# The four key quarters of the attention's sum, added by a TensorE fold or by an exchange through DRAM

## The chip, the cores and the metric

The kernel runs on one core of a Trainium2 chip. The metric is the time of one execution on the device, in microseconds (us). Engines are named as in the profile: PE is TensorE, DVE is VectorE, ACT is ScalarE, POOL is GpSimd, and SP is the engine that issues nearly all transfers. All data are float32. On PE each float32 matrix product shows in the trace as two passes, so a product of the program counts as two matmuls there.

## What is computed

One transformer block with adaptive layer norms, for 4 sequences of 1024 tokens, width 512, 16 heads of 32 with one shared key and value head (k_w and v_w have 32 rows), and a gated FFN of width 2048 with Walsh-Hadamard transforms:

```python
sa, ca, ga, sb, cb, gb = (silu(c) @ wmod) per sequence    # ga, gb kept away from zero
h = layernorm(x) * (1 + ca) + sa
q = (h @ q_w.T + q_b).reshape(b, s, 16, 32);  k = h @ k_w.T + k_b;  v = h @ v_w.T + v_b
attn = softmax(causal(q . k / 32 ** 0.5))
x = x + ga * ((attn @ v).reshape(b, s, 512) @ o_w.T + o_b)
h = layernorm(x) * (1 + cb) + sb
u = fwht(h * SU_ug) / 64
u = silu(u @ W_gate.T * wg) * (u @ W_up.T * wu)
x = x + gb * (fwht(u * SU_dp) / 64 @ W_down.T * wd)
```

## The kernel before

The 4096 tokens are handled in 8 blocks of 512 (half a sequence each), in the order given by `order`; a block is two halves of 256 tokens or four tiles of 128. For each block the attention side runs first norms, K, V and Q projections, scores, exponentials, transposes, the product with V, the output projection, the addition to x and the second norm; the FFN side then runs gate and up products (a Strassen form, L1054, with mixtures of the weights made on POOL, L1018) and down products (L1192) for that block. The FFN of one block runs beside the attention of the next ones.

No queue order is written by hand. Each part is a generator (a stream) that yields operations with an engine, a planned cost and the buffers that it reads and writes; `Flow` keeps a model of when each engine is free, and always emits the operation that could begin first, and among those of the same engine within 0.3 us the one with the lowest rank in the list at the end of `adaln_block` (L1234 ff.). Every engine then executes its instructions in the order in which they were emitted. So a changed cost, wait or rank changes the whole order. The model gives a transfer 3.9 us per MB, one after another, plus 1.5 us, and a change of PE's form (`mode`: full, rows, cols, tiles) 0.16 us.

The parts that the change touches:

- `fronts` projects K, V and Q from hT. `qT` holds the scaled Q^T of a whole block, 512 tokens (`[128, 4, 512]`). A half is projected when `st.scored >= (i - 1) * NT + 2 * (hf + 1)`, that is, when the same half of the block before has been used up (L416). The copies from PSUM are L428.
- `scores` (L500) makes the scores of a tile in row groups (each head's 32 channels lie on a quarter of the partitions); `minima` (L524, DVE), `exps` (L547, ACT), `reciprocals` (L561, DVE), `scales` (L581, ACT) and `turns` (L596, DVE transpose) follow.
- `attend` (L624) multiplies with V. The transpose leaves the keys of each group of 32 in place, so the product is made for each of four partition groups (quarters of the keys) by itself, in 32x32 tiles of PE, and comes out in four PSUM banks: 128 partitions = four groups of 32 channels for the four key quarters. ACT copies the four banks to `oT` (L637), a half tile (8 heads) at a time. There is one `oT`, and the copies of the next half tile wait for `st.folded >= qn`.
- `finish` adds the four key quarters: a product with `fold` (four stacked unit matrices, 128x32) in the four column groups of PE, L660, which also puts the heads on the partitions as the output projection needs them. ACT copies the result to `aT` (L663). After the second half tile comes the output projection (L297 with ow, aT), and DVE multiplies with the gate (L677).
- `add` (L692, L694) adds the gated result to x on POOL; from block 3 on, `transformed` does the first Walsh-Hadamard transform on POOL (L731).
- `load` (L286) issues all transfers on SP. The weights stream through small rings: wd three buffers, wu three, wg two, each 256 KB.

Of the kernel before, what the change touches and what calls it, by code (L numbers as in the profile page):

```python
# [17 lines left out]
H, HD = 16, 32  # L18
# [142 lines left out]
def adaln_block(ctx, tc, x_d, small_d, const_d, wmod_d, qwT_d, kwT_d, vwT_d, vb_d, owT_d, ob_d,  # L161
# [8 lines left out]


    ROWS, VIA_DRAM = 3, 4
    ps = psum.tile([P, 8, 512], F32, name="ps")

    def sb(name, *shape):
        return outer.tile([P, *shape], F32, name=name)
# [2 lines left out]
    wd_d = dram.tile([NFC, P, D], F32, name="wd_d")  # L179

    gates_d = dram.tile([5, B, D], F32, name="gates_d")
    xT_d = {"a": dram.tile([NHALF, D, HB], F32, name="xTa_d"), "f": dram.tile([NHALF, D, HB], F32, name="xTf_d")}
    rows = [slice(HD * j, HD * j + HD) for j in range(4)]

# [33 lines left out]
    vT = sb("vT", HB)  # L218
    vrep = sb("vrep", NKV * TB // 32, HD)
    hT = sb("hT", NDC, HB)  # L220
    qT = sb("qT", NDC, TB)

    bt = sb("bt", 7, 2, HB)
    B11, B12, B21, B22, T1, T2, T4 = range(7)
# [6 lines left out]
    NNM = 12  # L231
    nm = sb("nm", NNM, 2, 4)
    den = sb("den", 4, H)
    oT = sb("oT", 4, H // 2, 32)
    rden = sb("rden", 4, H)
    aT = sb("aT", NDC, P)
    ga, obga, y = sb("ga", D), sb("obga", D), sb("y", D)
# [43 lines left out]
    def until(queue, name):  # L281
        return lambda: bool(queue) or name in over
# [6 lines left out]
    def bk(b):  # L289
        return ("bank", b)  # L290

    def act_cost(n):
        return 0.285 + 0.00083 * n
# [95 lines left out]
    def fronts(blocks):  # L389
        for i in blocks:  # L390
            kv = kv_slot[order[i]]
            for hf in range(2):
                hh = 2 * i + hf
                yield lambda: st.first_normed > hh

                yield lambda: st.attended_blocks >= kv_behind[i]
                yield banks.have(1)
                o, = banks.take(1)
                yield Op("PE", mm(HB, 4), lambda: full_mm(
                    ps[:, o, 0:HB], [(kvw[:, k, :], hT[:, k, :]) for k in range(NDC)]),  # L400
                    [("hT", 0), ("hT", 2), "kw0", ("kw", 64), ("kw", 96)], [bk(o)], mode="full")
# [13 lines left out]

                yield lambda: st.scored >= (i - 1) * NT + 2 * (hf + 1)  # L416
                yield banks.have(2)
                bb = banks.take(2)
                for o, c0 in zip(bb, (0, 2)):
                    def products():  # L420
                        for c in (c0, c0 + 1):
                            full_mm(ps[:, o, (c - c0) * HB:(c - c0 + 1) * HB],
                                    [(qw[:, k, c * P:(c + 1) * P], hT[:, k, :]) for k in range(NDC)])
                    yield Op("PE", mm(HB, 8), products, [("hT", 0), ("hT", 2), "qw"], [bk(o)], mode="full")
                st.fronts = hh + 1
                for o, c0 in zip(bb, (0, 2)):
                    for c in (c0, c0 + 1):
                        yield Op("ACT", act_cost(HB), lambda: nc.scalar.activation(  # L428
                            qT[:, c, hf * HB:(hf + 1) * HB], ps[:, o, (c - c0) * HB:(c - c0 + 1) * HB], AF.Identity,
                            bias=qbs[:, c:c + 1], scale=HD ** -0.5), [bk(o)], [("qT", c, hf)])  # L430
                    banks.give(o)
                st.ready = hh + 1

# [53 lines left out]
    def scores():  # L487
        for u in units:
            yield lambda: st.ready > 2 * u.i + u.ql // 2
            yield lambda: st.attended >= u.behind  # L490

            for cs, kb, n in u.visits():
                yield lambda: len(to_min) < 2
                yield banks.have(4)
                bb = banks.take(4)

                def products():
                    for m, c in enumerate(cs):
                        for j, r in enumerate(rows):
                            nc.tensor.matmul(ps[:, bb[j], m * n:(m + 1) * n], qT[r, c, u.ql * P:(u.ql + 1) * P],  # L500
                                             kT[r, u.kv[kb] * TB:u.kv[kb] * TB + n], start=True, stop=True)
                yield Op("PE", mm(n, len(cs)) + 0.1, products,
                         [("qT", c, u.ql // 2) for c in cs] + [("kT", j) for j in u.half_keys(kb, n)],
                         [bk(b) for b in bb], mode="rows")
                to_min.append((u, cs, kb, n, bb))
            if u.h0 + u.heads == H:
                st.scored += 1
        over["scores"] = True
# [90 lines left out]
                to_attend.append(u)  # L599
        over["turns"] = True  # L600

    to_finish, to_add, to_norm, to_gate = deque(), deque(), deque(), deque()

    def attend():


        while True:
# [24 lines left out]
            for h0 in range(0, u.heads, 8):  # L632
                half = (u.h0 + h0) // 8
                qn = 2 * (u.i * NT + u.ql) + half
                yield lambda: st.folded >= qn
                for g in range(4):
                    yield Op("ACT", act_cost(HB), lambda: nc.scalar.copy(  # L637
                        oT[:, g], ps[:, bb[g], h0 * 32:h0 * 32 + HB].rearrange("p (h q) -> p h q", q=32)),
                        [bk(bb[g])], ["oT"])
                    if h0 + 8 == u.heads:  # L640
                        banks.give(bb[g])
                to_finish.append((u.i, u.ql, half))
            if u.h0 + u.heads == H and u.ql == NT - 1:
                st.attended_blocks = u.i + 1
        over["attend"] = True

    def finish():

        while True:
            yield until(to_finish, "attend")  # L650
            if not to_finish:
                break
            i, ql, half = to_finish.popleft()
            yield banks.have(1)
            bo, = banks.take(1)

            def folds():
                heads = oT.rearrange("p g (c j) q -> p j c g q", c=2)
                for j, r in enumerate(rows):
                    nc.tensor.matmul(ps[r, bo, 0:HB], fold, heads[:, j], start=True, stop=True)  # L660
            yield Op("PE", 0.5, folds, ["oT"], [bk(bo)], mode="cols")
            st.folded += 1
            yield Op("ACT", act_cost(HB), lambda: nc.scalar.copy(  # L663
                aT[:, 2 * half:2 * half + 2, :], ps[:, bo, 0:HB].rearrange("p (c q) -> p c q", c=2)), [bk(bo)], ["aT"])
            banks.give(bo)
# [12 lines left out]
            banks.give(o)  # L678
            to_add.append((i, ql))
        over["finish"] = True  # L680
# [550 lines left out]
    def early(rank, later):  # L1231
# [1 line left out]

    ranked = [  # L1234
        (0, copies), (0, sums), (0.5, multiply), (1, outputs), (0.2, load_weights_once), (2, load_jobs), (2, mods),
        (early(1.8, 3), attend), (early(1.8, 3), finish), (early(1.8, 3), add), (3.5, transformed), (early(2.2, 4), minima), (early(2.05, 4), scores), (early(1.7, 5), second_norms), (0, lambda: first_norms([0])), (0.1, lambda: first_norms([1])), (2.1, lambda: fronts([0])),
        (6.1, lambda: first_norms(range(2, NHALF))),
        (6, lambda: fronts(range(1, NBLK))), (early(2.3, 7), turns), (early(2.5, 8), exps), (1.5, reciprocals), (early(2.4, 7.5), scales), (2.6, butterflies),
        (2.15, transforms), (0.3, mixes), (9, hand_over), (10, lambda: load_gu("wu", 3, wupT_d)), (10, lambda: load_gu("wg", 2, wgT_d)), (10, load_wd),
# [54 lines left out]
```

## Time and profile before

| what | value |
|---|---|
| runs | 2073.97, 2070.32, 2072.89 us; median 2072.89 |
| profiled execution | 2072.41 us, of which the span of the core is 2070.6 |
| mean granted clock of PE | 0.993 of full speed |
| L660 (fold), PE | 512 matmuls, 41.3 us busy, 395 ns each |
| L663 (copy to aT), ACT | 64 copies, 24.5 us, 383 ns each |
| L637 (copies to oT), ACT | 256 copies, 78.5 us, 383 ns each |
| L624 (product with V), PE | 8256 matmuls, 196.5 us busy |
| L1192 (down), PE | 1024 matmuls, 480.9 us |
| L1054 (gate and up), PE | 3584 matmuls, 903.6 us |
| transfers | 226.8 MB, mean 110 GB/s; the packets of SP's queue took 37.3% of 16 engines' span |

Busy times are those of one profiled execution. An engine's busy share is an average over the span. "Idle before" a group is time in which its engine had nothing to do until the group began, with the instruction that ended it. The chain that ended last is followed back from the last instruction, at each step to what released it. A matmul row counts passes that overlap when they use different parts of PE, so the 512 fold matmuls of 395 ns each are busy for 41.3 us only.

### The profile page before, as it was taken

How to read it: one execution, taken by the hardware profiler on the slowest of the kernel's cores; microseconds unless marked ns; L12 is line 12 of the kernel's file. 1: busy time of each engine (PE TensorE's matmuls, PEld its weight loads, DVE VectorE, ACT ScalarE, POOL GpSimd, SP SyncE). 2: the span in 40 equal slices, each digit the busy share in tenths (PEclk: the TensorE clock that was granted, in tenths of full speed). 3: DMA queues.
4: the chain of work that ended last, by engine and by line, in shares of the span. 5: the costliest groups of instructions: out<-in, count | busy, mean ns of one | idle time of the engine just before them, and what ended most of it. 6: DMA issues, size and time to landing. Idle time of an engine off the chain costs nothing.

```text
span 2070.6 us, 41956 instructions
## 1 busy us (share of the span) xinstructions
PE 1992.2 (96%) x16168; PEld 1272.1 (61%) x16168; DVE 1361.6 (66%) x3131; ACT 1150.5 (56%) x2447; POOL 863.1 (42%) x1134
## 2 busy tenths in 40 slices
PE   6898999999999999999999999999899999999998
PEld 4466666556665665646666566665566646664774
DVE  4985666676773776767875787775866758772331
ACT  3756765566664774646654675567744646650220
POOL 2582333223331455533563155252665346254441
PEclk9899999999999999999999999999999999999999
DMA  6145423432233453343333642243433344235333
GB/s 211 40 141 152 129 82 92 115 116 73 77 98 112 134 126 101 104 140 107 84 90 99 167 114 89 70 133 100 125 82 87 93 123 123 68 92 163 107 104 114
DMA packets 328144, 226.77 MB, mean 110 GB/s; under 512 B 108020, under 2 KB 266868, under 8 KB 327944
## 3 DMA queue, kind: packets, MB, share of 16 engines
q1 hardware_dynamic: 324008, 221.65, 37.3%
q8 instruction: 128, 2.10, 0.4%
q10 hardware_dynamic: 3936, 2.43, 0.4%
q14 instruction: 72, 0.59, 0.1%
HBM read 191.47 MB, written 32.55 MB: 108 GB/s over the span
## 4 chain that ended last, share of the span: by engine, by line
PE 86%; DVE 5%; DMA 3%; issue 2%; POOL 2%; SPq 1%; ACT 0%; ACTq 0%; POOLq 0%; DVEq 0%
PE ps L1054 36%; PE ps L1192 19%; PE ps L297 11%; PE ps L624 9%; PE ps L500 7%; PE ps L660 2%; DVE p L596 1%; DVE p L524 1%; POOL u L731 1%; DMA raw<-in_wmod 1%; PE ps L962 1%; POOL xr L731 1%; DVE g L1167 1%; SPq L286 1%; PE ps L965 1%
## 5 line engine op out<-in xcount | busy, mean ns | idle before, releaser
L1192 PE MATMUL ps<-wd,g 128*128 128x512 f32 x1024 | 480.9, 604 | 12.1 <-DVE g L1167 9.1
L547 ACT ACTIVATE p<-p,nm 128x512 f32<-128x512 f32 (+7 forms) x512 | 390.9, 766 | 25.9 <-DVE nm L524 25.5
L1054 PE MATMUL ps<-bt,ws 128*128 128x256 f32 x1536 | 380.4, 384 | 7.0 <-DVE rden L561 4.6
L581 ACT ACTIVATE p<-p,rden 128x640 f32<-128x640 f32 (+7 forms) x480 | 349.5, 783 | 39.0 <-DVE rden L561 38.3
L596 DVE STREAM_TRANSPOSE p<-p 128x512 f32<-128x512 f32 (+7 forms) x256 | 341.3, 1357 | 41.1 <-ACT p L581 38.4
L1141 DVE TENSOR_TENSOR s<-ps,s 128x256 f32<-128x256 f32 x384 | 159.8, 420 | 266.6 <-PE ps L1054 201.3
L1054 PEld LDWEIGHTS ps<-bt,ws 128*128 128x128 f32 x1536 | 290.4, 191 | 68.6 <-issue 16.6
L1192 PEld LDWEIGHTS ps<-wd,g 128*128 128x128 f32 x1024 | 185.0, 189 | 237.8 <-issue 186.2
L524 DVE CUSTOM_DVE_ANT_0 p<-ps,maskw 128x512 f32<-128x512 f32 (+3 forms) x512 | 276.6, 581 | 53.0 <-PE ps L500 52.2
L1018 POOL TENSOR_TENSOR ws<-wu 128x256 f32<-128x256 f32 x128 | 103.8, 811 | 476.6 <-DMA wu<-in_wupT 461.5
L1054 PE MATMUL ps<-bt,wu 128*128 128x256 f32 x1024 | 270.9, 387 | 1.0 <-issue 0.7
L1054 PE MATMUL ps<-bt,wg 128*128 128x256 f32 x1024 | 252.3, 383 | 3.4 <-issue 3.4
L1054 PEld LDWEIGHTS ps<-bt,wu 128*128 128x128 f32 x1024 | 188.0, 190 | 92.1 <-issue 49.2
L1054 PEld LDWEIGHTS ps<-bt,wg 128*128 128x128 f32 x1024 | 193.3, 191 | 59.6 <-issue 30.6
L624 PE MATMUL ps<-p,vrep 32*32 32x256 f32 (+1 forms) x8256 | 196.5, 415 | 20.4 <-issue 11.4
L1157 ACT ACTIVATE th<-s,wgh 128x512 f32<-128x512 f32 x128 | 92.4, 722 | 178.5 <-DVE g L1167 103.1
L500 PE MATMUL ps<-kT,qT 32*128 32x512 f32 (+3 forms) x1536 | 177.1, 528 | 1.4 <-ACT vT L409 1.4
L624 PEld LDWEIGHTS ps<-p,vrep 32*32 32x32 f32 x8256 | 120.7, 103 | 92.9 <-issue 40.2
L1132 ACT COPY s<-ps 128x256 f32<-128x256 f32 x128 | 47.5, 371 | 221.2 <-PE ps L1054 220.9
L637 ACT COPY oT<-ps 128x256 f32<-128x256 f32 x256 | 78.5, 383 | 137.3 <-PE ps L624 121.2
L1018 POOL TENSOR_TENSOR ws<-ws,wg 128x256 f32<-128x256 f32 x128 | 101.0, 789 | 114.8 <-DMA wg<-in_wgT 93.7
L694 POOL TENSOR_TENSOR xr<-xr,y 128x512 f32<-128x512 f32 x32 | 43.0, 1344 | 242.2 <-DVE y L677 238.6
(117 smaller groups left out, 2345.1 us busy)
## 6 DMA issues: line engine op xcount, KB each, us to landing
wd<-wd_d SPq DMA_DIRECT2D x256, 256.0 KB, 2.6
wu<-in_wupT SPq DMA_DIRECT2D x128, 256.0 KB, 2.9
wg<-in_wgT SPq DMA_DIRECT2D x128, 256.0 KB, 3.2
xr<-in_x SPq DMA_DIRECT2D x32, 256.0 KB, 3.1
x_d<-xr SPq DMA_DIRECT2D x32, 256.0 KB, 2.0
xo<-x_d SPq DMA_DIRECT2D x32, 256.0 KB, 3.8
out<-xo SPq DMA_DIRECT2D x32, 256.0 KB, 2.4
xn<-in_x SPq DMA_DIRECT2D x30, 256.0 KB, 3.4
```

The source lines that it names most:

```text
L297: nc.tensor.matmul(out, l, r, start=(k == 0), stop=(k == len(pairs) - 1))
L500: nc.tensor.matmul(ps[:, bb[j], m * n:(m + 1) * n], qT[r, c, u.ql * P:(u.ql + 1) * P], kT[r, u.kv[kb] * TB:u.kv[kb] * TB + n], start=True, ...
L524: yield Op("DVE", 0.245 + 0.00103 * n, lambda: nc.vector.tensor_tensor_reduce(o, ps[:, bb[j], k * n:(k + 1) * n], m, -1.0, nm[:, slot, 0, ...
L547: yield Op("ACT", act_cost(u.kmax) + 0.19, lambda: nc.scalar.activation(e, e, AF.Exp, bias=nm[:, slot, u.t, j:j + 1], scale=-1.0, accum_ou ...
L581: yield Op("ACT", act_cost(u.kmax), lambda: nc.scalar.activation(e, e, AF.Copy, scale=r), [("rden", ds, c)], [u.key(h)])
L596: yield Op("DVE", 0.135 + 0.00105 * 2 * u.kmax, lambda: nc.vector.transpose(e, e), [], [u.key(h), u.key(h + 1)])
L624: nc.tensor.matmul(ps[rows[c], bb[g], 0:w], vrep[rows[g], v0 + c, :], pv[rows[g], :, k:k + 32], start=(kt == 0), stop=(kt == nkt - 1))
L1018: yield Op("POOL", 0.66, lambda: getattr(nc.gpsimd, "tensor_" + e)(a[o][0], a[x][0], a[y][0]), [a[n][1] for n in (x, y) if n != "A21" or o ...
L1054: nc.tensor.matmul(o, w[:, c, :], bt[:, t, c, :], start=start and c == 0, stop=stop and c == 1, skip_group_check=True)
L1141: yield Op("DVE", 0.43, lambda: nc.vector.tensor_add(s[:, j, :], ps[:, bank, half * HB:(half + 1) * HB], s[:, j, :]), [bk(bank)], [sk[j]])
L1157: yield Op("ACT", act_cost(512), lambda: nc.scalar.activation(th, s[:, 0:2, :], AF.Tanh, scale=wgh[:, f:f + 1]), [sk[0], sk[1]], ["th"])
L1192: nc.tensor.matmul(ps[:, acc[j], :], g[:, j * P:(j + 1) * P], ff["wd"][:, m % NWD, :], start=(f == 0), stop=(f == NFC - 1))
```

## The change

From the second block on, the four key quarters are no longer added by PE. The copies of ACT write `oT` as [key quarter and channel, head group j, (c, g, q)]; each half tile of `oT` (512 KB) is written to DRAM (`o_d`), and read back with partition groups and head groups exchanged, by four transfers of 128 KB, one for each group of 32 partitions, so that the four key quarters lie beside one another on the same partition. POOL then adds them in two steps (1024 to 512 to 256 elements per partition), the second of which writes `aT`. The output projection is as before. Block 0 keeps the fold.

`oT` becomes two half tiles, and the copies wait only for the half tile before the last one. To make room, `qT` holds 256 tokens in place of 512, and the Q projection of a half waits until all scores of the halves before it have been made. The new stream `exchange` has rank 2.9.

```diff
+    EXCHANGED = 1
+    o_d = dram.tile([2, P, 4, HB], F32, name="o_d")
-    qT = sb("qT", NDC, TB)
+    qT = sb("qT", NDC, HB)
-    oT = sb("oT", 4, H // 2, 32)
+    oT = sb("oT", 2, 4, HB)
...
-                yield lambda: st.scored >= (i - 1) * NT + 2 * (hf + 1)
+                yield lambda: st.scored >= 2 * hh
...
-                            qT[:, c, hf * HB:(hf + 1) * HB], ps[:, o, (c - c0) * HB:(c - c0 + 1) * HB], AF.Identity,
-                            bias=qbs[:, c:c + 1], scale=HD ** -0.5), [bk(o)], [("qT", c, hf)])
+                            qT[:, c, :], ps[:, o, (c - c0) * HB:(c - c0 + 1) * HB], AF.Identity,
+                            bias=qbs[:, c:c + 1], scale=HD ** -0.5), [bk(o)], [("qT", c)])
...
-                yield lambda: st.folded >= qn
+                yield lambda: st.folded >= qn - 1
+                o = oT[:, half].rearrange("p j (c g q) -> p g c j q", c=2, g=4)
                 for g in range(4):
                     yield Op("ACT", act_cost(HB), lambda: nc.scalar.copy(
-                        oT[:, g], ps[:, bb[g], h0 * 32:h0 * 32 + HB].rearrange("p (h q) -> p h q", q=32)),
-                        [bk(bb[g])], ["oT"])
+                        o[:, g], ps[:, bb[g], h0 * 32:h0 * 32 + HB].rearrange("p (c j q) -> p c j q", c=2, q=32)),
+                        [bk(bb[g])], [("oT", half)])
...
-                to_finish.append((u.i, u.ql, half))
+                (to_finish if u.i < EXCHANGED else to_exchange).append((u.i, u.ql, half))
...
+    def exchange():
+        while True:
+            yield until(to_exchange, "attend")
+            if not to_exchange:
+                break
+            i, ql, half = to_exchange.popleft()
+            o, key = oT[:, half], ("oT", half)
+            yield load(0.5, o_d[half], o, [("o_d", half)], [key])
+            for j, r in enumerate(rows):
+                yield load(0.125, o[r], o_d[half].rearrange("(c d) j x -> j d c x", c=4)[j], [key], [("o_d", half)])
+            o = o.rearrange("p c x -> p (c x)")
+            yield Op("POOL", 1.3, lambda: nc.gpsimd.tensor_add(o[:, 0:512], o[:, 0:512], o[:, 512:1024]), [], [key])
+            yield Op("POOL", 0.66, lambda: nc.gpsimd.tensor_add(
+                aT[:, 2 * half:2 * half + 2, :].rearrange("p c q -> p (c q)"), o[:, 0:HB], o[:, HB:512]), [key], ["aT"])
+            st.folded += 1
+            to_finish.append((i, ql, half))
+        over["exchange"] = True
...
-            yield banks.have(1)
-            bo, = banks.take(1)
-            def folds():
-                heads = oT.rearrange("p g (c j) q -> p j c g q", c=2)
-                for j, r in enumerate(rows):
-                    nc.tensor.matmul(ps[r, bo, 0:HB], fold, heads[:, j], start=True, stop=True)
-            yield Op("PE", 0.5, folds, ["oT"], [bk(bo)], mode="cols")
-            st.folded += 1
+            if i < EXCHANGED:
+                yield banks.have(1)
+                bo, = banks.take(1)
+                def folds():
+                    for j, r in enumerate(rows):
+                        nc.tensor.matmul(ps[r, bo, 0:HB], fold, oT[:, half, j, :], start=True, stop=True)
+                yield Op("PE", 0.5, folds, [("oT", half)], [bk(bo)], mode="cols")
+                st.folded += 1
...
-        (early(1.8, 3), attend), (early(1.8, 3), finish), (early(1.8, 3), add), (3.5, transformed), (early(2.2, 4), minima), (early(2.05, 4), scores), (early(1.7, 5), second_norms), (0, lambda: first_norms([0])), (0.1, lambda: first_norms([1])), (2.1, lambda: fronts([0])),
+        (early(1.8, 3), attend), (early(1.8, 3), finish), (2.9, exchange), (early(1.8, 3), add), (3.5, transformed), (early(2.2, 4), minima), (early(2.05, 4), scores), (early(1.7, 5), second_norms), (0, lambda: first_norms([0])), (0.1, lambda: first_norms([1])), (2.1, lambda: fronts([0])),
```

More of the change, by code (lines that the diff above doesn't have):

```diff
@@ L499, in products @@
                         for j, r in enumerate(rows):
-                            nc.tensor.matmul(ps[:, bb[j], m * n:(m + 1) * n], qT[r, c, u.ql * P:(u.ql + 1) * P],
+                            nc.tensor.matmul(ps[:, bb[j], m * n:(m + 1) * n], qT[r, c, u.ql % 2 * P:(u.ql % 2 + 1) * P],
                                              kT[r, u.kv[kb] * TB:u.kv[kb] * TB + n], start=True, stop=True)
                 yield Op("PE", mm(n, len(cs)) + 0.1, products,
-                         [("qT", c, u.ql // 2) for c in cs] + [("kT", j) for j in u.half_keys(kb, n)],
+                         [("qT", c) for c in cs] + [("kT", j) for j in u.half_keys(kb, n)],
                          [bk(b) for b in bb], mode="rows")
@@ L600, in turns @@
         over["turns"] = True
-    to_finish, to_add, to_norm, to_gate = deque(), deque(), deque(), deque()
+    to_exchange, to_finish, to_add = deque(), deque(), deque()
     def attend():
@@ L645, in attend @@
         over["attend"] = True
+    def exchange():
[15 more added lines that the diff above has]
+        over["exchange"] = True
     def finish():
         while True:
-            yield until(to_finish, "attend")
+            yield lambda: bool(to_finish) or "attend" in over and "exchange" in over
             if not to_finish:
@@ L653, in finish @@
             i, ql, half = to_finish.popleft()
-            yield banks.have(1)
-            bo, = banks.take(1)
-            def folds():
-                heads = oT.rearrange("p g (c j) q -> p j c g q", c=2)
-                for j, r in enumerate(rows):
-                    nc.tensor.matmul(ps[r, bo, 0:HB], fold, heads[:, j], start=True, stop=True)
-            yield Op("PE", 0.5, folds, ["oT"], [bk(bo)], mode="cols")
-            st.folded += 1
-            yield Op("ACT", act_cost(HB), lambda: nc.scalar.copy(
-                aT[:, 2 * half:2 * half + 2, :], ps[:, bo, 0:HB].rearrange("p (c q) -> p c q", c=2)), [bk(bo)], ["aT"])
-            banks.give(bo)
+            if i < EXCHANGED:
[6 more added lines that the diff above has]
+                st.folded += 1
+                yield Op("ACT", act_cost(HB), lambda: nc.scalar.copy(
+                    aT[:, 2 * half:2 * half + 2, :], ps[:, bo, 0:HB].rearrange("p (c q) -> p c q", c=2)), [bk(bo)], ["aT"])
+                banks.give(bo)
             if half == 0:
```

## The prediction, made before the changed kernel was run

> **What bounds the kernel now.** I read the page first (busy shares, the 40 slices, the chain that ended last), then the waits, then the chain piece by piece between 900 and 960 us, then the groups that the change touches.
>
> ```profile
> span 2070.6 us, 41956 instructions
> ...
> PE 1992.2 (96%) x16168; PEld 1272.1 (61%) x16168; DVE 1361.6 (66%) x3131; ACT 1150.5 (56%) x2447; POOL 863.1 (42%) x1134
> ...
> PE   6898999999999999999999999999899999999998
> ...
> PE 86%; DVE 5%; DMA 3%; issue 2%; POOL 2%; SPq 1%; ACT 0%; ACTq 0%; POOLq 0%; DVEq 0%
> ```
>
> The third line is the one to look at: from the fifth slice (about 205 us) on, PE is busy 90% or more in nearly every slice. The chain of waits (fourth line) is matmuls for 86% of the span; what is not PE lies mostly in the first 200 us. Between 300 and 1800 us the windows view has PE busy for 1468.5 of 1500 us. So in the long middle the kernel lasts as long as its matmuls do, and a matmul taken out there is time taken out, as long as nothing new makes PE wait.
>
> The chain in that stretch shows what the fold costs (start, length, what):
>
> ```profile
> 919.18 0.80 PE ps L624 x33
> 919.98 1.91 PE ps L1192 x4
> 921.89 1.08 PE ps L500 x16
> 922.97 0.57 PE ps L660 x8
> 923.54 3.63 PE ps L1192 x8
> ...
> 947.47 1.72 PE ps L1192 x4
> 949.19 6.04 PE ps L1054 x28
> 955.23 1.72 PE ps L1192 x4
> ```
>
> L660 is the fold: 0.57 us on the path, no gap before or after. Compare the two lengths of L1192 x4: 1.72 us behind another full 128x128 matmul (L1054), 1.91 us behind L624, which uses the array in 32x32 tiles. A change of the array's form therefore costs the next group 0.19 us (L1192 x8 at 3.63 behind the fold, where 8 at 0.43 would be 3.44, says the same). The fold, in four column groups, is a form of its own, and whatever follows it pays; its own entry is inside its 0.57.
>
> **The change part by part.** The sum is made against the profiled execution, 2072.4 us (span 2070.6, 1.8 around it); the median of the runs is 2072.9, 0.5 above it.
>
> *Folds removed.* The fold stays for block 0 (8 of 64 half tiles); 56 go. 56 x 0.57 = 31.9 us of PE. In the order of the changed program's instructions the changes of form on PE go from 516 to 427: 89 fewer. 56 of them are the folds' own entries, already counted; the other 33 x 0.19 = 6.3 us. Together **-38.2 us**. All of it lies on the path by the chain above. The 56 copies to aT on ACT (L663, 383 ns each) go too: 21 us of an engine at 56%, no one's bound, counted at nothing.
>
> *Exchange added.* Per half tile one 512 KB write and four 128 KB reads: 280 DMA issues on SP (941 become 1221; at 0.34 to 0.5 us, 95 to 140 us of a queue that mostly waits) and 58.7 MB on top of 226.8. Then two POOL additions.
>
> ```profile
> L660 PE MATMUL ps<-oT,fold 128*32 128x256 f32 x512 | 41.3, 395 | 7.8 <-DVE g L1167 6.8 <-ACT p L547 1.0
> ...
> L692 POOL TENSOR_TENSOR xr<-xr,obga 128x512 f32<-128x512 f32 x32 | 43.1, 1348 | 25.1 <-DMA xr<-in_x 24.7 <-DVE gt L885 0.4
> ...
> L1018 POOL TENSOR_TENSOR ws<-wu 128x256 f32<-128x256 f32 x128 | 103.8, 811 | 476.6 <-DMA wu<-in_wupT 461.5 <-PE ps L624 8.7 <-PE ps L1054 5.2
> ```
>
> The reader is to see POOL's price and its slack. The additions are of the shapes of L692 (1.35 us) and L1018 (0.64 to 0.81 across POOL's 256-wide rows, I take 0.73): 2.1 us each time, 116 us in all, POOL from 42% to 47%. Behind them on POOL stand the weight mixtures (L1018), and there POOL idles 461.5 us until wu lands, 3.6 us per chunk: the additions fit into that, with no cost on average.
>
> The way through DRAM is long. Write: between 2.0 us for 256 KB (x_d<-xr) and 5.1 for 1 MB (wd_d<-wo), 3.0 us. Four issues: 1.9 us. Last read: between 2.1 us (64 KB) and 3.2 (256 KB), 2.5 us. Additions 2.1. Sum 9.5 us where fold and copy took 1.0. What hides it: in the new order I added up PE's work, by the rows' durations, between a tile's last attention product (L624) and its output projection (L297 with ow). Before, the median is 6 us; after, in the 28 tiles of blocks 1 to 7, it is 18 to 61 us, median 25. So PE has other work for twice the latency, and two oT buffers in place of one let the next half tile be copied meanwhile: 0 us. Without that cover it would be 28 tiles x 9 us = 250 us.
>
> *SP's queue and the transfers.* This is the cost that no row shows. SP issues in order: the first read waits for its write, and behind it stand loads of weights. In the new order on average 3.6 loads of wd, wu or wg stand between a write and its last read, and in 12 of 56 cases the read follows the write directly, so that SP stands still for the whole 3.0 us.
>
> ```profile
> PEld ps L1192 <- issue: 186.2, 705, 0.8
> ...
> PEld ps L1192 <- DVE g L1167: 25.8, 30, 1.7
> ...
> PEld ps L1192 <- DMA wd<-wd_d: 13.6, 29, 1.5
> ```
>
> The third line, from the waits (total, times, longest): today the down products wait 13.6 us for wd at their weight load, and 2.7 more at the matmul, 34 waits in all, beside 256 loads. The low end is below nothing: a PSUM bank fewer is held per fold, and the last block's attention ends earlier against the other work (in the order, 102 gate/up and 50 down matmuls are left behind the last attention product, before 2 and 34), which can win back the 4 us that PE idles between 1800 and 1900: -4. The high end: each exchange holds one load up by 2 us (the rows above give 4.1 us per MB, so 0.5 MB takes 2.0) with no spare buffer, at the write and at the reads: 56 x 4 = 224 us. Down products come in runs (two wd per 3.4 us against 2.6 us of landing) only in part of a block; elsewhere a wd is used every 8 us and a load may be 5 us late. So I take the end that is near the row of today: 16.3 us of waits grow by half, **+8 us**.
>
> *Q^T of half a block.* Q for a half block may be written only when the last scores of the half before are taken. The burst of 32 passes (twice 3.45 us in the chain near 150 us) and its ACT copies leave VectorE without scores for some 9 us, 15 times. PE fills that with FFN work, which is at hand from the first gate product (186 us) on: 0; with no filler it would be 135 us. Before the first gate product the new order has 16 Q and 4 K/V matmuls fewer (40 passes, 8.6 us), which move from the start into the full part. Where PE is the bound in the start (the transforms of wd, 100 to 170 us), they bring the start forward and cost nothing, else 8.6: **+2 us**.
>
> *VectorE beside POOL.* L1159 takes 693 ns at the median and up to 1764, L1162 486 and up to 1316: such an instruction stretches by about one POOL instruction when it meets one. Excess of the means now: 128 x (70 + 110) ns = 23 us at 863 us of POOL; 13% more POOL gives 3 us more, between 0 and 56 x 1.1 = 60. I take **+3 us**, near the rows. [...]
>
> Sum: 2072.4 - 38.2 + 8 + 2 + 3 = **2047 us**, -1.2%. The new order itself can move PE's idle time (31.5 us between 300 and 1800) by some 10 us either way.
>
> **The rivals.**
>
> *SP's queue takes the gain and more (slower).* The loads behind each read come late and PE waits for wd or for mixtures. With 5 us for the other terms it decides from (38.2 - 5) / 56 = 0.6 us per exchange; at 1.0 us the time is 2072.4 - 33.2 + 56 = 2095. For it: 201 of the 512 weight loads stand inside an exchange, and wd has three buffers. Against it: POOL and SP idle today mostly for buffers that PE still holds. 0.15.
>
> *The gate chain on VectorE is held by the additions (slower).* All 56 pairs of additions stretch an L1159 or L1162 by 1.1 us, and PE waits for each: 2072.4 - 28.2 + 60 = 2104; against the 28.2 that is left without this term it decides from 0.5 us each. PE waits 34.9 us in 45 waits for L1167 today, but VectorE is idle for 34% of the span. [...] 0.03.
>
> *Half of the gain is lost* to new waits, 0.3 to 0.5 us per exchange: 2060 to 2068. 0.12.
>
> *The folds go and the time stays.* The attention chain (scores, exponentials, transposes) would be the bound, and PE's freed time idle: 2072, give or take 4. For it: before, FFN work has nearly run out when the last attention product comes. Against: PE at 97.9% in the middle. 0.06.
>
> *More than forecast*, the waits shrink: below 2027. 0.02.
>
> **How the numbers follow.** The forecast's own band, 2027 to 2060, has 0.62. A measurement of this kernel can tell about 0.2% (4 us) from no change. Faster: 0.62 + 0.12 + 0.02 = 0.76; same 0.06; slower 0.15 + 0.03 = 0.18. The range 2027 to 2080 takes in the forecast, the half gain, no change and the mild end of the slow cases.
>
> **What would show it.** L660 at 64 matmuls instead of 512 and PE's busy time near 1954 us; PE's chain share as before. SP's term is right if waits of L1192 for wd stay under 25 us, wrong if they or L1018's waits for oT's reads pass 40 us on PE's side. POOL should stand at about 980 us, and the waits of aT's additions should be on reads of o_d, not in the chain. A first gate product after 195 us would show the start mis-sized; L1159 and L1162 means above 900 and 750 ns would show VectorE's.

## The result, and the profile after

| | median of the runs, us | ratio to the kernel before, 95% interval |
|---|---|---|
| before, beside the changed kernel | 2073.43 (2070.32 to 2076.73) | 1 |
| changed kernel | 2051.64 (2046.40 to 2053.72) | 0.9891 [0.9866, 0.9915] |
| changed kernel again, beside the second set of experiments | 2050.59 (2048.97 to 2052.40), before 2076.43 | 0.9890 [0.9875, 0.9905] |

The forecast was 2047, in a range of 2027 to 2080. One run of 2110.6 us at a granted clock of 0.938, of the kernel with 1/16 of the bytes below, counts in that kernel's median but not in its ratio. The profiled execution of the changed kernel took 2046.40 us, the shortest of its runs; its span is 2044.6. Line numbers move: L660 is L684 now, L1192 is L1216, L1054 is L1078, L1162 is L1186, L1167 is L1191, L297 is L300, L500 is L503; L664 and L665 are the two additions.

From the page of the changed kernel:

```profile
span 2044.6 us, 41680 instructions
...
PE 1955.1 (96%) x15720; PEld 1264.7 (62%) x15720; DVE 1376.8 (67%) x3131; ACT 1133.5 (55%) x2391; POOL 973.5 (48%) x1246
...
PE   6997999999999999999999999998999999999998
...
PE 85%; DVE 5%; DMA 5%; issue 2%; POOL 2%; SPq 1%; ACT 0%; POOLq 0%; ACTq 0%; DVEq 0%
```

PE's busy time fell from 1992.2 to 1955.1 us, by 37.1. The span fell by 26.0. So PE idles 89.5 us in place of 78.4: 11.1 us of the gain were given back as new idle time. By its idle time the kernel is nearly as much PE's as before; in the chain DMA's share rose from 3 to 5%.

The chain between 900 and 960 us no longer holds a fold:

```profile
921.71 1.07 PE ps L503 x8
922.78 3.63 PE ps L1216 x8
926.41 0.86 PE ps L503 x8
927.27 3.63 PE ps L1216 x8
...
941.89 3.65 PE ps L300 x8
...
946.40 1.28 POOL xr L718
...
947.70 4.09 DMA x_d<-xr
```

Scores (L503, in row groups) and down products (L1216, full array) follow each other; each down group still pays for the change of form (3.63 us for 8 matmuls, where 8 at the 0.43 of before would take 3.44), but the third form between them is gone. From 945.5 to 961.4 us the chain runs through DVE, POOL and a transfer, which it did not before; PE idles 1.2 us between 940 and 970, so little of that is lost.

The additions and the transfers (groups and DMA issues of the page; the last column of an issue is its median time to landing):

```profile
L664 POOL TENSOR_TENSOR oT<-oT 128x512 f32<-128x512 f32 x56 | 73.4, 1311 | 170.6 <-DMA oT<-o_d 138.2
L1042 POOL TENSOR_TENSOR ws<-wu 128x256 f32<-128x256 f32 x128 | 105.8, 827 | 365.6 <-DMA wu<-in_wupT 309.2
...
wd<-wd_d SPq DMA_DIRECT2D x256, 256.0 KB, 2.8
...
o_d<-oT SPq DMA_DIRECT2D x56, 512.0 KB, 3.8
oT<-o_d SPq DMA_DIRECT2D x224, 128.0 KB, 3.4
```

POOL waited 138 us for the reads, in 17 waits, and its wait for wu shrank by about as much, from 461.5 to 309.2 us. Write and read land 0.8 and 0.9 us later than the prediction took from the rows of before (3.0 and 2.5). From the waits of PE's weight loads and of PE (total, times, longest; two views, one after the other):

```profile
PEld ps L1216 <- DVE g L1191: 34.7, 34, 2.1
PEld ps L1216 <- DMA wd<-wd_d: 22.9, 29, 8.0
```

```profile
PE ps L1216 <- DVE g L1191: 16.7, 23, 1.2
...
PE ps L1216 <- DMA wd<-wd_d: 10.5, 7, 7.1
```

Waits for wd went from 16.3 to 33.4 us in sum, 7 to 8 of it in one wait; waits of the down products for L1191, DVE's last gate instruction, from 34.9 to 51.4. Before, though, the fold waited 11.2 us for that instruction as well, so the growth is 5 us rather than 17. (The same wait can appear in both views.) The start is the other place. The first two stretches of 100 us of the windows view, before and after (stretch, its length, busy time of PE, PEld, DVE, ACT, POOL with the number of instructions, then PE's granted clock, DMA share, GB/s):

```profile
0.00:100.00 100.00, 77.57 (x680) 46.35 (x680) 64.54 (x222) 60.59 (x186) 38.26 (x50) 0.93 0.42 128
100.00:200.00 100.00, 91.28 (x754) 63.10 (x755) 72.89 (x160) 58.74 (x155) 57.29 (x44) 0.97 0.48 138
```

```profile
0.00:100.00 100.00, 75.89 (x583) 47.65 (x588) 59.91 (x190) 50.59 (x151) 44.76 (x48) 0.93 0.56 170
100.00:200.00 100.00, 82.43 (x838) 49.31 (x808) 71.08 (x184) 70.69 (x203) 49.72 (x41) 0.88 0.34 100
```

Between 100 and 200 us PE is busy 8.9 us less, and at a lower clock. The first gate product begins at 191.3 us (before: 186.4), and until then PE idles 39.0 us (before: 30.3). Nearly all new idle time is in the first 200 us, where PE idles 41.7 us in place of 31.2; behind them it idles 47.8 us in place of 47.3. So what the waits for wd and L1191 grew by, other waits fell by.

### The profile page after: what moved, and what is told of

Its sections match the earlier page's. It is cut to its first block, busy times and chain, and to the rows that moved or that the text cites. A ratio compares the mean times of both kernels' runs of the same rounds, so it can differ in the third digit from the quotient of the medians.

```text
span 2044.6 us, 41680 instructions
## 1 busy us (share of the span) xinstructions
PE 1955.1 (96%) x15720; PEld 1264.7 (62%) x15720; DVE 1376.8 (67%) x3131; ACT 1133.5 (55%) x2391; POOL 973.5 (48%) x1246
## 4 chain that ended last, share of the span: by engine, by line
PE 85%; DVE 5%; DMA 5%; issue 2%; POOL 2%; SPq 1%; ACT 0%; POOLq 0%; ACTq 0%; DVEq 0%
PE ps L1078 36%; PE ps L1216 19%; PE ps L300 11%; PE ps L627 9%; PE ps L503 7%; DMA wd<-wd_d 1%; DMA raw<-in_wmod 1%; SPq L289 1%; DVE p L599 1%; DVE p L527 1%; PE ps L986 1%; PE ps L989 1%; DMA x_d<-xr 1%; DVE s L1165 1%; DVE g L1191 0%
## 5 line engine op out<-in xcount | busy, mean ns | idle before, releaser
L1216 PE MATMUL ps<-wd,g 128*128 128x512 f32 x1024 | 482.3, 605 | 27.4 <-DVE g L1191 16.7
L1078 PE MATMUL ps<-bt,ws 128*128 128x256 f32 x1536 | 378.3, 382 | 2.8 <-DVE bt L808 1.9
L1216 PEld LDWEIGHTS ps<-wd,g 128*128 128x128 f32 x1024 | 185.6, 190 | 258.4 <-issue 189.9
L1078 PEld LDWEIGHTS ps<-bt,ws 128*128 128x128 f32 x1536 | 289.6, 191 | 58.8 <-issue 13.6
L1042 POOL TENSOR_TENSOR ws<-wu 128x256 f32<-128x256 f32 x128 | 105.8, 827 | 365.6 <-DMA wu<-in_wupT 309.2
L1078 PE MATMUL ps<-bt,wu 128*128 128x256 f32 x1024 | 269.0, 385 | 0.0
L1078 PE MATMUL ps<-bt,wg 128*128 128x256 f32 x1024 | 250.9, 381 | 0.4 <-DVE g L1191 0.3
L1078 PEld LDWEIGHTS ps<-bt,wu 128*128 128x128 f32 x1024 | 189.6, 190 | 83.0 <-issue 39.0
L1078 PEld LDWEIGHTS ps<-bt,wg 128*128 128x128 f32 x1024 | 192.8, 190 | 56.2 <-issue 24.3
L503 PE MATMUL ps<-kT,qT 32*128 32x512 f32 (+3 forms) x1536 | 175.6, 530 | 1.5 <-DVE nm L527 1.4
L664 POOL TENSOR_TENSOR oT<-oT 128x512 f32<-128x512 f32 x56 | 73.4, 1311 | 170.6 <-DMA oT<-o_d 138.2
L1042 POOL TENSOR_TENSOR ws<-ws,wg 128x256 f32<-128x256 f32 x128 | 96.9, 757 | 112.0 <-DMA wg<-in_wgT 84.7
```

The lines of the kernel that those rows point to most:

```text
L1042: yield Op("POOL", 0.66, lambda: getattr(nc.gpsimd, "tensor_" + e)(a[o][0], a[x][0], a[y][0]), [a[n][1] for n in (x, y) if n != "A21" or o ...
L1078: nc.tensor.matmul(o, w[:, c, :], bt[:, t, c, :], start=start and c == 0, stop=stop and c == 1, skip_group_check=True)
L1216: nc.tensor.matmul(ps[:, acc[j], :], g[:, j * P:(j + 1) * P], ff["wd"][:, m % NWD, :], start=(f == 0), stop=(f == NFC - 1))
```

## The experiments

The kernel before had medians of 2073.4, 2077.8, 2076.4 and 2079.1 us beside the four sets of runs, each set on one chip. So kernels are compared by their ratio to the kernel before in the same set; 0.001 is 2.07 us. The runs' medians are in the table behind the last experiment.

**Is the fold's PE time on the path?** The kernel before without 56 of its folds, in the same order.

```diff
-                for j, r in enumerate(rows):
+                for j, r in enumerate(rows if i == 0 else ()):
                     nc.tensor.matmul(ps[r, bo, 0:HB], fold, heads[:, j], start=True, stop=True)
...
-                aT[:, 2 * half:2 * half + 2, :], ps[:, bo, 0:HB].rearrange("p (c q) -> p c q", c=2)), [bk(bo)], ["aT"])
+                aT[:, 2 * half:2 * half + 2, :],
+                (ps[:, bo, 0:HB] if i == 0 else oT[:, 0:2].rearrange("p g h q -> p (g h q)")[:, 0:HB]).rearrange(
+                    "p (c q) -> p c q", c=2)), [bk(bo)], ["aT"])
```

> The kernel before, in its own order of instructions, with the 56 folds of blocks 1 to 7 left out: ACT copies the first two of the four parts of oT to aT in place of the folded sum, so the four key quarters are not added there and the output is not the block's. Nothing else is added. Theory (PE's matmuls are the bound, a fold costs 0.57 us and its neighbours' changes of form 0.19): 2073 - 38 = 2035, between 2029 and 2042, PE busy about 1955. Rival (the attention chain is the bound and PE's freed time idles): 2060 or more, with PE's busy time down by the same 37 us. Second rival (only the matmuls' own 0.43 us count, no cost of form): about 2049.

Measured: ratio 0.9862 [0.9841, 0.9883], about -29 us: between the theory's 38 and the 24 of the second rival. PE's busy time fell to 1958.1 us, by 34; its idle time rose from 78.4 to 84.8. The interval (24 to 33 us) reaches both ranges, so the time alone does not decide on a price of the changes of form; PE's busy time does, for it fell by more than the 56 x 0.43 = 24 us of the matmuls alone. The attention chain is not the bound. Waits took part of the rest (views for PE and for PE's weight loads; L1194 is the down product, L1169 the gate instruction here):

```profile
PE ps L1194 <- DVE g L1169: 18.3, 26, 1.1
```

```profile
PEld ps L1194 <- DVE g L1169: 38.1, 39, 1.7
```

Before, these were 9.1 and 25.8, and the fold itself stood 6.8 and 4.4 us waiting for the same instruction. The two sums over fold and down product grow by 2.4 and 7.9 us. A reading that fits, and that no run isolates: where a fold stood between gate and down product, the down product now comes sooner to an operand that comes no sooner. In the changed kernel, whose order is new, the same waits stand at 16.7 and 34.7.

**Do the bytes of the exchange cost?** The changed kernel in its own order, each transfer cut to 1/16:

```diff
-            yield load(0.5, o_d[half], o, [("o_d", half)], [key])
+            yield load(0.5, o_d[half][:, :, 0:16], o[:, :, 0:16], [("o_d", half)], [key])
...
-                yield load(0.125, o[r], o_d[half].rearrange("(c d) j x -> j d c x", c=4)[j], [key], [("o_d", half)])
+                yield load(0.125, o[r, :, 0:16], o_d[half].rearrange("(c d) j x -> j d c x", c=4)[j][:, :, 0:16], [key], [("o_d", half)])
```

> The changed kernel in its own order, all 280 issues of the exchange in place, but each transfer moves only 16 of every 256 elements (1/16 of the bytes), so blocks 1 to 7 add mostly numbers that were not exchanged. Theory (the exchange's cost is its bytes and its landing times, which hold up wd, whose waits rose from 16 to 33 us): 2034 to 2044, wd waits back under 20 us, landing of wd from 2.8 to 2.6 us. Rival (the issues and waits in SP's order cost, not the bytes): 2048 to 2054. Second rival (neither costs; PE's new idle time is in the start and in the new order): 2048 to 2054 as well, but then the wd waits fall while the span doesn't.

Measured: 0.9833 [0.9812, 0.9854], 0.006 below the changed kernel, 12 us, between some 6 and 18 with both intervals. The size is that of the first theory. Its mechanism isn't shown: the wd waits stand at 19.9 and 9.0 us, little under the 22.9 and 10.5 of the changed kernel and over the 20 that was expected, and the long one is still there (view of PE's weight loads):

```profile
PEld ps L1216 <- DMA wd<-wd_d: 19.9, 27, 8.0
```

In the changed kernel that load is issued at 1425.3 us and lands 7.0 us later. Two broadcasts of gate rows are issued just ahead of it and two loads of bt behind it; reads of the exchange are issued 2.1 us ahead and 0.4 us behind. Since the wait stays with 1/16 of the exchange's bytes, these bytes do not make it; which transfer does isn't shown. The edit also shortens the way through DRAM: the write lands in 2.8 us in place of 3.8, the reads in 2.6 in place of 3.4. The profiled execution took 2048.2 us, 5 over the median of its runs, so its trace doesn't tell where the others were faster. This stays open.

**Do POOL's additions cost?** The same order, both additions cut to 16 elements:

```diff
-            yield Op("POOL", 1.3, lambda: nc.gpsimd.tensor_add(o[:, 0:512], o[:, 0:512], o[:, 512:1024]), [], [key])
+            yield Op("POOL", 1.3, lambda: nc.gpsimd.tensor_add(o[:, 0:16], o[:, 0:16], o[:, 512:528]), [], [key])
...
-                aT[:, 2 * half:2 * half + 2, :].rearrange("p c q -> p (c q)"), o[:, 0:HB], o[:, HB:512]), [key], ["aT"])
+                aT[:, 2 * half:2 * half + 2, :].rearrange("p c q -> p (c q)")[:, 0:16], o[:, 0:16], o[:, HB:HB + 16]), [key], ["aT"])
```

> The changed kernel in its own order, with the two POOL additions of each half tile cut from 512 and 256 to 16 elements per partition, so that blocks 1 to 7 get almost no sum. Theory (the additions fit into POOL's idle time and cost VectorE about 3 us): 2046 to 2052, POOL busy about 870 us. Rival (POOL's additions hold the mixtures, or VectorE's gate instructions that meet them): 2040 or less, with L1186's mean falling from its value in the changed kernel to that of before.

Measured: 0.9850 [0.9829, 0.9871], 0.004 below the changed kernel: 8 us, between some 3 and 14 with both intervals. (The 2048.0 us would be the theory's; beside a kernel before of 2077.8, the changed kernel would take some 2055.) The groups show the fall of L1186's mean that was named (mean ns behind the busy time). First before, then changed, then with short additions:

```profile
L1162 DVE SCALAR_TENSOR_TENSOR g<-th,cg,s 128x256 f32<-128x256 f32 x128 | 76.3, 596 | 4.5
```

```profile
L1186 DVE SCALAR_TENSOR_TENSOR g<-th,cg,s 128x256 f32<-128x256 f32 x128 | 84.9, 663 | 4.5
```

```profile
L1186 DVE SCALAR_TENSOR_TENSOR g<-th,cg,s 128x256 f32<-128x256 f32 x128 | 77.1, 603 | 4.5
```

In this trace L1186 takes 67 ns longer on average than L1162 did before, and with short additions 60 of the 67 are gone. The size varies: over all kernels here the mean is 596 to 630 ns without full additions and 619 to 688 with them (633 in the changed kernel's second profile). L1183 (L1159 before), which the prediction counts too, shows no clear stretch: 760 to 793 ns without and 741 to 810 with them. That this stretch makes the 8 us is not shown: PE's waits for L1191 fell only from 16.7 and 34.7 to 14.9 and 32.9 us, and the edit also takes 1.6 us off each half tile's way to aT and 87 us off POOL.

**What does Q^T of half a block cost?** The kernel before with that edit alone:

```diff
-    qT = sb("qT", NDC, TB)
+    qT = sb("qT", NDC, HB)
...
-                yield lambda: st.scored >= (i - 1) * NT + 2 * (hf + 1)
+                yield lambda: st.scored >= 2 * hh
...
```

> The kernel before with Q^T of half a block alone: qT of 256 tokens and the later Q projection, folds on PE, one oT. Theory (the start pays for it: in the changed kernel PE idles 39.0 us before the first gate product against 30.3 before, and the middle does not): 2078 to 2084, with most of the difference before 200 us. Rival (the longer start comes from the other parts of the change, such as two oT buffers, and the half is free): 2071 to 2076. Second rival (the half starves VectorE of scores 15 times): over 2090, with PE idle spread over the span.

Measured: 1.0206 [1.0183, 1.0229], +43 us, far over the theory. It is not only the start (first gate product at 195.3 us): PE idles 109.8 us in all, 31 more than before, 10 of them in the first 200 us and 21 spread over the rest. That is the second rival by its number; VectorE's waits for scores grew by 10 us only (70.3 to 80.5), so whether that is the whole cause is not shown. And the same edit with the second oT, folds on PE:

```diff
-    EXCHANGED = 1
+    EXCHANGED = 8
```

> The changed kernel with the exchange put off beyond the last block (EXCHANGED = 8): all 64 folds on PE, Q^T of half a block, but two oT buffers. Beside Q^T of half a block alone (ratio 1.0206, +43 us). Theory (the half needs a second oT to be cheap, since one oT and late Q projections hold up the same attention chain): 2080 to 2095. Rival (the half costs 43 us wherever the folds are, and it is the exchange that pays for it): 2110 or more, PE busy about 2012 and idle over 100 us.

Measured: 1.0060 [1.0046, 1.0073], +12 us; as the theory had it: with the second oT the half is cheap. Idle time 86.1 us. From here to the changed kernel the way of adding differs, and with it the planned order: 1.0060 to 0.9890, -35 us.

**Does each exchange bring its part?** Exchange from block 4 on (`EXCHANGED = 4`), and from block 0 on (`EXCHANGED = 0`):

> The changed kernel with the exchange from block 4 on (EXCHANGED = 4): half of the 64 half tiles folded on PE, half exchanged. Between none exchanged (ratio 1.006) and 56 exchanged (0.989). Theory (each exchange takes its fold's 0.6 to 0.7 us off PE, evenly): 1.006 - 32/56 x 0.017 = 0.996, that is 2064 to 2072 where the kernel before has 2076. Rival (the gain comes from one stage, such as the end, where more FFN work is left behind the last attention product): near 0.989 or near 1.006.

> The changed kernel with block 0 exchanged too (EXCHANGED = 0). Theory (the start is a chain of waits, in which 8 folds of PE time are worth nothing and 8 times 9 us of latency are paid once or twice): 2055 to 2075. Rival (the cover holds in the start as well, and 8 folds more leave PE): 2044 to 2049.

Measured: 0.9965 [0.9950, 0.9980] for 32 exchanges, as the theory had it. 0.0095 for the first 32 is 0.61 us each, 0.0075 for the next 24 is 0.65 us each: even within some 0.2 us each, and next to the 38.2 / 56 = 0.68 us that the prediction took off PE. But each of these kernels has an order of its own, and the last experiments show that an order alone can move the time by as much as these steps. With block 0 the ratio is 1.0134 [1.0117, 1.0151], 50 us over the changed kernel, more than either expected. Its first gate product begins at 251 us, 60 later than in the changed kernel; until then PE idles 57.7 us and is granted 0.84 of its clock. From that window's waits of PE:

```profile
PE ps L503 <- ACT qT L431: 6.7, 2, 6.4
...
PE ps L300 <- POOL aT L665: 4.3, 1, 4.3
```

In the start there is no FFN work to lay over the round trip, and the output projection waits for POOL's addition. That wait is 4.3 us; the new idle time there is 19 us, and the rest of the 60 is PE busy for 41 us longer, at a granted clock of 0.84 where the changed kernel has 0.91 up to its first gate product.

**Is the second oT needed for the exchange?** The changed kernel with one oT and Q^T of a whole block, as before:

```diff
-    qT = sb("qT", NDC, HB)
+    qT = sb("qT", NDC, TB)
...
-    oT = sb("oT", 2, 4, HB)
+    oT = sb("oT", 1, 4, HB)
...
-                yield lambda: st.folded >= qn - 1
+                yield lambda: st.folded >= qn
...
```

> The changed kernel with the buffers as before: Q^T of a whole block and one oT, and the exchange from block 1 on. Theory (the half is what costs, the latency of the exchange is hidden): 2015 to 2035, the ratio of the fold left out alone (0.986) or better. Rival (one oT is held for the 10 us through DRAM, the copies of the next half tile and so the banks of the product with V wait): 2060 or more, with PE's idle time up and ACT's copies to oT waiting for POOL's additions.

Measured: 1.0483 [1.0468, 1.0497], +100 us, and 123 over the changed kernel: the rival. ACT's copies (first view, ACT) wait for POOL's addition, and PE's products with V and gate products wait as well (second view, PE):

```profile
ACT oT L641 <- POOL aT L665: 86.8, 19, 20.0
```

```profile
PE ps L1078 <- DVE bt L808: 33.3, 4, 21.0
PE ps L627 <- DVE p L599: 20.3, 9, 7.2
```

PE idles 163 us. The gate products run out of normed blocks (bt), which no row of the other kernels shows at such length (8.8 us at most).

**Who issues the write, and who decides the order?** Write on ACT's queue, planned so; then the same write by ACT, but planned as if SP issued it, so that PE, DVE and POOL keep the changed kernel's order; then another rank for the exchange.

The first line is that of the changed kernel, the next two stand in its place in one run each; the last two lines are the third run's, cut from the list of ranks.

```diff
-            yield load(0.5, o_d[half], o, [("o_d", half)], [key])
+            yield load(0.5, o_d[half], o, [("o_d", half)], [key], q=nc.scalar)
+            yield Op("SP", 0.5, lambda: nc.scalar.dma_start(o_d[half], o), [key], [("o_d", half)], mb=0.5)
...
-        (2.9, exchange)
+        (0.4, exchange)
```

> The changed kernel with the write to DRAM issued from ACT's queue, right behind the copies that it needs, in place of SP's; the reads stay on SP. The order is planned anew. Theory (SP standing still for ACT's copies, 50 us in 14 waits, and for the write, 48 us in 23 waits, holds up wd): 2040 to 2047, wd waits of PE under 25 us. Rival (these waits cost nothing, bytes and order do): 2048 to 2056. The bound on the other side: ACT spends 56 x 0.5 us more, at 55% busy: nothing.

> The changed kernel with the write to DRAM issued by ACT, but planned as if SP did, so that the order on PE, VectorE and POOL is that of the changed kernel. Beside the write on ACT's queue in an order of its own (ratio 1.0016, 29 us over the changed kernel). Theory (the new order made that slow, not the issuing engine): 2044 to 2056. Rival (56 issues on ACT and their place behind its copies cost the 29 us): 2070 or more, with PE waiting for ACT.

> The changed kernel with rank 0.4 for the exchange in place of 2.9, so that its transfers and additions go ahead of nearly all others when they could begin together; 422 changes of form on PE in place of 427, 152 gate/up matmuls left behind the last attention product in place of 102. Theory (the exchange is covered as it is, its rank moves only the order): 2035 to 2065, either way. Rival (the loads of weights behind SP's reads decide): 2065 or more, with wd waits of PE over 50 us.

Measured: 1.0016 [1.0003, 1.0029] planned for ACT, 26 us over the changed kernel by the ratios and against both expectations; 0.9859 [0.9839, 0.9878] in the old order, some 6 us better than the changed kernel (1 to 12 with both intervals), and the best of the kernels here that compute the whole block; 0.9961 [0.9947, 0.9976] with rank 0.4, 15 us over it: the 2070.2 us are outside the theory's range and inside the rival's, but the rival's mechanism is not there (wd waits of 15.9 and 3.9 us, less than in the changed kernel). The write lands in 3.0 us from ACT's queue (old order) and in 3.8 from SP's. So ACT as the issuing engine cost no time in this run, and the order did: two edits that add no work change the time through the new order, by 15 us (rank) and 33 us (ACT, planned so or not).

| kernel | median, us | beside before | span of the profile | PE busy | PE idle | mean granted clock |
|---|---|---|---|---|---|---|
| before | 2073.4 | | 2070.6 | 1992.2 | 78.4 | 0.993 |
| changed | 2051.6 | 2073.4 | 2044.6 | 1955.1 | 89.5 | 0.989 |
| folds left out | 2047.7 | 2077.8 | 2042.9 | 1958.1 | 84.8 | 0.993 |
| 1/16 of the bytes | 2043.6 | 2077.8 | 2046.4 | 1957.9 | 88.5 | 0.988 |
| short additions | 2048.0 | 2077.8 | 2047.1 | 1960.2 | 86.9 | 0.987 |
| Q^T of half a block alone | 2120.7 | 2077.8 | 2124.1 | 2014.3 | 109.8 | 0.982 |
| changed, again | 2050.6 | 2076.4 | 2047.5 | 1955.4 | 92.1 | 0.990 |
| none exchanged | 2085.4 | 2076.4 | 2081.4 | 1995.3 | 86.1 | 0.989 |
| one oT, whole Q^T | 2173.4 | 2076.4 | 2171.1 | 2008.1 | 163.0 | 0.966 |
| write planned for ACT | 2079.7 | 2076.4 | 2076.3 | 1969.4 | 106.9 | 0.986 |
| exchange from block 4 | 2072.3 | 2079.1 | 2070.2 | 1984.1 | 86.1 | 0.987 |
| exchange from block 0 | 2107.9 | 2079.1 | 2107.8 | 1992.8 | 115.0 | 0.975 |
| write by ACT, order kept | 2048.8 | 2079.1 | 2047.3 | 1951.5 | 95.8 | 0.992 |
| exchange at rank 0.4 | 2070.2 | 2079.1 | 2062.5 | 1962.4 | 100.1 | 0.992 |

## Why the prediction was right, step by step

- **Folds removed, -38.2 us: right in kind.** PE's busy time fell by 37.1 us, and by 40 from the kernel with none exchanged to the changed one; the ladder of 0, 32 and 56 exchanges gives 0.61 and 0.65 us each net, against 0.68 without any new wait, each step in a new order. In an unchanged order, leaving out the folds alone gave only 29 us: PE's busy time fell by 34, and its idle time rose by 6, in part in waits for L1167, which the prediction didn't consider. (It counts 34.9 us of such waits; with those of the fold they were 46.1.)
- **Latency of the exchange, 0 us: near enough behind a second buffer, and not tested by itself.** The prediction put a price of 250 us on the lost cover; with one oT (and Q^T of a whole block) 123 us are lost. The cover is the second buffer as much as PE's other work. Where there is no other work, in block 0, 8 exchanges and the order that comes with them cost 50 us. Behind two buffers in blocks 1 to 7 a small price stays possible: the runs with fewer bytes and with short additions shorten the way too, by some 1.8 and 1.6 us per half tile, and both were faster.
- **SP's queue and the transfers, +8 us: the size fits, the place isn't shown.** 12 us (6 to 18) by the run with 1/16 of the bytes. The waits for wd doubled (16.3 to 33.4 us) where half more was said, between the prediction's mark for right (25) and for wrong (40), and with 1/16 of the bytes they fell by 4.5 us only.
- **VectorE beside POOL, +3 us: the stretch is there, its size too small.** The run with short additions gives 8 us (3 to 14), not all of it surely VectorE's. The prediction scaled the stretch of L1159 and L1162 by POOL's busy time, 13% more; in the profile of the changed kernel the stretch of the two grew by 128 x (36 + 67) ns = 13 us where 3 were expected, and the short additions take 128 x (18 + 60) ns = 10 us of it back; the part of L1159 is within its spread. The prediction's stretch by about one POOL instruction is the longest case (L1159: 1764 ns at a median of 693, with a mean of 763). Why the stretch grew by more than POOL's busy time did is not shown.
- **Q^T of half a block, +2 us: mis-sized.** It costs 12 us with the second oT, 43 without, each in an order of its own. Of the two cases "they bring the start forward and cost nothing, else 8.6" the prediction leaned to the wrong one: PE idles 8.7 us more before the first gate product (9.2 with none exchanged), the whole of what was moved away.
- **Not in the sum: PE's clock.** It fell from 0.993 to 0.989. As an estimate, (1 - clock) x span is 14.5 us before and 22.5 after, 8 us of the difference; by the same estimate PE's work at full clock fell by 45. These are two single executions: over the runs of the second set the mean clock is 0.991 before and 0.989 in the changed kernel, by the same estimate 4 us.
- **The sum, -25 us: near, but not for its own reasons alone.** In the profiled executions, 11.1 us of new idle time stand against the 13 us of new costs, and 37.1 of PE against 38.2. But 10.5 of the 11.1 lie in the first 200 us, for which the prediction had 2; behind them idle time grew by 0.5, where it had 11 for SP and VectorE. The parts, each measured by itself, do not add up: -29 for the folds, +12 for Q^T, +12 for the bytes and +8 for the additions make +3 us, and -22 was measured. They were measured in different orders and can overlap; what makes up the difference is not shown.
- The rivals: the queue of SP at 1.0 us per exchange, half of the gain lost and a time that stays are ruled out by the result itself (22 of 25 us gained), VectorE held for 60 us by the run with short additions. (For half of the gain lost, 0.3 us per exchange gives 2072.4 - 33.2 + 17 = 2056 by the prediction's own sum, not 2060.)

One reading was too kind: that another order of the same work can move the time by 15 to 33 us (rank 0.4; planned for ACT against ACT in the old order) was priced at 10. The changed kernel's order happens to be a good one; that the forecast came within 5 us is in part luck.

## What to carry to other kernels

Where one engine is busy nearly all the time (here PE, 96% of the span), count for a piece of work taken off it its time on the path and the changes of form around it, less what it may have been covering (38.2 us were counted here, 29 measured with the folds left out). Moving it through DRAM was cheap here only behind a second buffer and beside other work: the same exchange gained 23 us with two buffers and lost 100 with one, against the kernel before, and 8 exchanges more in block 0, with the order that comes with them, cost 50. When a planner lays out the order, compare an edit in the old order too, or its effect and that of the new order can't be told apart.

## What the runs showed of the hardware that was not expected

In the kernel with the most idle time on PE its busy time was longer too. The kernel with one oT runs the same matmuls as the changed one, with 390 changes of form in place of 427; PE idles 163.0 us in place of 89.5, and yet is busy 53 us longer. The last column of the table goes with it (0.966 and 0.989 of the clock); in the stretch from 400 to 500 us of the run with one oT, PE idles 17.6 us and is granted 0.85 of its clock:

```profile
400.00:500.00 100.00, 82.43 (x903) 48.11 (x914) 70.67 (x172) 61.17 (x115) 31.31 (x36) 0.85 0.38 114
500.00:600.00 100.00, 97.83 (x927) 66.43 (x902) 71.24 (x152) 60.22 (x102) 34.94 (x46) 1.00 0.35 104
```

Busy time less (1 - clock) x span, an estimate of PE's work at full clock, takes that difference away (1934 and 1933 us) and sorts the kernels by their folds: 1972 to 1978 us with all 64 (before, Q^T half alone, none exchanged), 1957 with 32, 1932 to 1946 with 8 or none. Single matmuls of the gate and up products take up to 717 ns in the changed kernel and 767 before, where the median is 379 in both: about twice as long. Much idle time and a lower clock do not stand together everywhere in the table: with the exchange at rank 0.4 PE idles 100.1 us at a mean clock of 0.992. What lowers the granted clock is not shown by these runs.
